# Perceiver block: time mixing in steps inside the attention of later batches, inverse square roots by power, first exponentials between score tiles

## Chip, cores and metric

The kernel runs on one core of a Trainium2 chip, in fp32. The metric is the device time of one execution in microseconds (us), the median of several runs. The engines are named as the profile names them: PE is TensorE (PEld its weight loads), DVE is VectorE, ACT is ScalarE, POOL is GpSimd, SP is SyncE, which here only issues DMAs. A line such as L357 is a line of the kernel before.

## The reference

A block of three residual parts over x, 32 batches of 64 tokens of 256 channels, with a context of 1601 keys of 192 channels for each batch. With LN a layer norm without weights (divide by the square root of the variance plus 1e-5):

```python
# 1. cross attention, 16 heads of 64
q = LN(x) @ w_q;  k, v = split(context @ w_kv)
x = x + softmax(q k^T / 8) v @ w_out + b_out
# 2. time mixing over the 64 tokens of a batch
z = LN(x);  s = z shifted by one token, zero first
k = (z*mix_k + s*(1-mix_k)) @ Wk.T      # v and r alike, with their own mix and weight
r = sigmoid(r)
td = exp(-exp(time_decay))
for t:                                   # num, den start at zero
    e   = exp(time_first + k_t)
    w_t = (num + e*v_t) / (den + e)
    num = td*num + exp(k_t)*v_t;  den = td*den + exp(k_t)
x = x + (r * w) @ Wo.T + bo
# 3. feed-forward, 1024 wide
x = x + relu(LN(x) @ w1 + b1) @ w2 + b2
```

## The kernel before

**Setup.** x is held in SBUF as 16 tiles of 128 tokens (two batches each, `x_sb`). The key projection is folded into the queries, so that scores are taken against the raw context: `queries` normalises x, multiplies by `w_q` and by the transposed key weights, and stores the folded queries to `q_dram` by SyncE (L233, L239) in four groups. The time-mixing weights are transposed (`rw_T`, L317). Nine small loads of biases and per-channel vectors (`bias_rows`, `cols`, `b1_sb`, L303 to L311) are issued by GpSimd.

**Attention** runs over 64 halves u = 2b + j, one batch b and eight heads j at a time, so that a half has 512 query columns. `scores` computes six tiles `s_ps` of 128 x 2 x 512 in PSUM (two buffers, L350) and a rest `s_ps_r` (L369); ScalarE copies each to `s_sb` (L357), VectorE keeps a running maximum (L359, L361). `hooks` are functions called after a given score tile. `max_all` reduces the maximum over partitions on GpSimd (L387), `exps` subtracts it on VectorE (L393) and takes exponentials on ScalarE (L396). `Half.total` sums the exponentials (VectorE, then GpSimd, L427); `inverse` turns the sums into reciprocals (L437 to L441). `av_lo` and `av_hi` multiply the exponentials by the raw context, low 128 channels (L450, `o_lo`) and high 64 (L462, L472, `o_hi`); `out` scales them (L488). After every fourth half, `vproj` applies the value weights (L504) and the output projection (L515) for one tile of 128 tokens and adds to `x_sb` (L522, L523).

The loop is a software pipeline written out by hand: TensorE's queue for half u is the score tiles of u, then `av_lo` of u-1, then `av_hi` of u-1. The previous half's inverse is the hook after score tile 3, `vproj` the hook after tile 1. The engines work through their queues in order; a scheduler places the instructions of different streams in each queue. Four halves, with one `vproj`, form a period; there are 16.

**The tail** starts when attention is done. It works on four blocks of 512 tokens. `rwkv(nb)` is the time mixing of a block: `normed` (statistics on VectorE, square root on ScalarE, reciprocal, and eight transposes, L599), the shifted copy `xp` (L607), for k, v and r a scaled copy `tmp` on ScalarE (L618) and a product-and-add `in_k`, `in_v`, `in_r` on VectorE (L621), the projections (L630) with N=512, exponentials (L651) and a sigmoid (L658), 32 scans per block (L663), the reciprocal of the denominator (L670), products (L671, L672) and the output product `ry` (L677). `ffn(nb)` is the feed-forward: `h_ps` (L698), relu, `fy` (L710), two adds (L718, L719) and the output DMA (L720). The order is written out:

```python
    rwkv(0)
    for nb in range(NB):
        if nb + 1 < NB:
            rwkv(nb + 1)
        ffn(nb)
```

The inverse square root of the norms is

```python
    def rstd_of(dst, var):
        nc.vector.tensor_scalar(dst, var, EPS, None, ALU.add)
        nc.scalar.activation(dst, dst, AF.Sqrt)
        nc.vector.reciprocal(dst, dst)
```

Of the kernel before, what the change touches and what calls it, by code (L numbers as in the profile page):

```python
# [9 lines left out]
F32 = mybir.dt.float32  # L10
# [10 lines left out]
def kernel(  # L21
# [33 lines left out]

    nc = tc.nc
# [27 lines left out]
    nc.gpsimd.memset(ones, 1.0)  # L84

# [11 lines left out]
    def rstd_of(dst, var):  # L97
        nc.vector.tensor_scalar(dst, var, EPS, None, ALU.add)
        nc.scalar.activation(dst, dst, AF.Sqrt)
        nc.vector.reciprocal(dst, dst)  # L100
# [12 lines left out]
    with tc.tile_pool(name="aw", bufs=1) as aw:  # L113
        wv_lo = aw.tile([P, INNER], F32, name="wv_lo")
        wv_hi = aw.tile([P, INNER], F32, name="wv_hi")
        wo_sb = aw.tile([P, INNER // P, D], F32, name="wo_sb")

        with ExitStack() as st_a:
            cpool = st_a.enter_context(tc.tile_pool(name="ctx", bufs=1))

            kp = st_a.enter_context(tc.tile_pool(name="keys", bufs=2))
# [140 lines left out]
            with tc.tile_pool(name="setup", bufs=1) as sp, tc.tile_pool(  # L262
# [20 lines left out]
                for n, w in (("Wk", Wk), ("Wv", Wv), ("Wr", Wr), ("Wo", Wo)):  # L283
                    nats[n] = sp.tile([P, 2, D], F32, name=f"nat_{n}")
                    nc.sync.dma_start(nats[n], w.rearrange("(c p) h -> p c h", p=P))
                for g in range(NP // 2):
# [14 lines left out]

                for n, v in enumerate((b_out, bo, b2)):
                    nc.gpsimd.dma_start(bias_rows[:, n, :], v.partition_broadcast(P))  # L303
                with nc.allow_non_contiguous_dma(reason="per-channel vectors"):
                    for n, v in enumerate((time_decay, time_first)):
                        nc.gpsimd.dma_start(cols[:, n, :], v.rearrange("(c p) -> p c", p=P))
                    for n, v in enumerate((mix_k, mix_v, mix_r)):
                        nc.gpsimd.dma_start(
                            cols[:, 2 + n, :], v.rearrange("a b (c p) -> p (a b c)", p=P)
                        )  # L310
                    nc.gpsimd.dma_start(b1_sb, b1.rearrange("(c p) -> p c", p=P))  # L311
# [20 lines left out]
            ap = st_a.enter_context(tc.tile_pool(name="attn", bufs=1))  # L332
            ps_s = st_a.enter_context(tc.tile_pool(name="ps_s", bufs=2, space=PSUM))
            ps_o = st_a.enter_context(tc.tile_pool(name="ps_o", bufs=1, space=PSUM))
            ps_m = st_a.enter_context(tc.tile_pool(name="ps_m", bufs=2, space=PSUM))

            def bank(shape, name):
                return ps_m.tile(shape, F32, tag="m", name=name)

# [50 lines left out]
            def exps(u, s_sb, mb):  # L390
                for i in range(KC // 4):
                    s4 = s_sb[:, 4 * i : 4 * i + 4, :]
                    nc.vector.tensor_tensor(  # L393
                        s4, s4, mb.unsqueeze(1).to_broadcast([P, 4, HALF]), ALU.subtract
                    )
                    nc.scalar.activation(s4, s4, AF.Exp)  # L396
                sr = s_sb[0:KR, KC, :]
                nc.vector.tensor_tensor(sr, sr, mb[0:KR, :], ALU.subtract)
                nc.scalar.activation(sr, sr, AF.Exp)

            class Half:
# [27 lines left out]
                def inverse(self):  # L429
# [10 lines left out]
                    self.rden = ap.tile([P, HALF // BL, BL], F32, tag="rden", name=f"rden_{u}")  # L440
# [89 lines left out]
            oT = None  # L530
            for u in range(2 * B):
                b, j = divmod(u, 2)

                hooks = {}
                if late is not None:
                    hooks[1] = [late.vproj]
                if last is not None:
                    hooks[3] = [last.inverse]

                if last is not None:  # L540
                    last.total()
# [7 lines left out]
                exps(u, s_sb, mb)  # L549
                if j == 0 and b + 1 < B:  # L550
                    cT_next = ctx_prep(b + 1)
                elif j == 1:
                    cT = cT_next
                if last is not None:
                    last.av_hi()
                    last.out()
                if j == 0:
                    c_tiles[b] = ctx_load(b)
# [4 lines left out]
            late.vproj()  # L563
            last.total()
            last.inverse()
            last.av_lo(0, NCK)
            last.av_hi()
# [3 lines left out]
    NB = 4  # L571
    TB = NT * P // NB
    BB = TB // T
    TT = TB // P
    NF = FF // P
    wp = ctx.enter_context(tc.tile_pool(name="fw", bufs=1))
    rp = ctx.enter_context(tc.tile_pool(name="rw", bufs=1))
    fp = ctx.enter_context(tc.tile_pool(name="ff", bufs=2))
    pp_t = ctx.enter_context(tc.tile_pool(name="pp_t", bufs=2, space=PSUM))
    pp_m = ctx.enter_context(tc.tile_pool(name="pp_m", bufs=4, space=PSUM))  # L580
    pp_y = ctx.enter_context(tc.tile_pool(name="pp_y", bufs=2, space=PSUM))

    w1_sb = wp.tile([P, 2, FF], F32, name="w1_sb")
    w2_sb = wp.tile([P, NF, D], F32, name="w2_sb")
    nc.sync.dma_start(w1_sb, w1.rearrange("(c p) f -> p c f", p=P))
    nc.sync.dma_start(w2_sb, w2.rearrange("(c p) d -> p c d", p=P))

    def normed(nb, name, dst):
        tiles = [nb * TT + k for k in range(TT)]
        mv, rstd = stats_of(fp, tiles, f"{name}_{nb}")  # L590
        xn = fp.tile([P, TT, D], F32, tag="xn", name=f"xn_{name}_{nb}")
        for k, i in enumerate(tiles):
            nc.vector.tensor_scalar(
                xn[:, k, :], x_sb[:, i, :], mv[:, k, 0:1], rstd[:, k : k + 1], ALU.subtract, ALU.mult
            )
        for c in range(2):
            pt = pp_t.tile([P, TT, P], F32, tag="t", name=f"xT_{name}_{nb}_{c}")
            for k in range(TT):
                nc.tensor.transpose(pt[:, k, :], xn[:, k, c * P : (c + 1) * P], ident)  # L599
            dst(c, pt)  # L600

    def rwkv(nb):
        xp = rp.tile([P, 2, BB, T + 1], F32, tag="xp", name=f"xp_{nb}", bufs=2)
        nc.gpsimd.memset(xp[:, :, :, 0:1], 0.0)

        def put(c, pt):
            nc.scalar.copy(  # L607
                xp[:, c, :, 1 : T + 1], pt.rearrange("p k (b t) -> p (k b) t", t=T)
            )

        normed(nb, "ln2", put)

        mixed = []
        for n, nm in enumerate(("k", "v", "r")):
            tmp = rp.tile([P, 2, BB, T], F32, tag="tmp", name=f"tmp_{nm}_{nb}", bufs=2)
            mi = rp.tile([P, 2, BB, T], F32, tag=f"in_{nm}", name=f"in_{nm}_{nb}", bufs=2)
            for c in range(2):
                nc.scalar.activation(  # L618
                    tmp[:, c], xp[:, c, :, 0:T], AF.Copy, scale=omm[:, n, c : c + 1]
                )  # L620
                nc.vector.scalar_tensor_tensor(  # L621
                    mi[:, c], xp[:, c, :, 1 : T + 1], cols[:, 2 + n, c : c + 1], tmp[:, c],
                    ALU.mult, ALU.add,
                )
            mixed.append(mi.rearrange("p c b t -> p c (b t)"))

        def proj(src, w, c, nm):
            ps = pp_m.tile([P, TB], F32, tag="mm", name=f"{nm}_ps_{nb}_{c}")
            for hc in range(2):
                nc.tensor.matmul(  # L630
                    ps,
                    lhsT=rw_T[w][:, hc, c * P : (c + 1) * P],
                    rhs=src[:, hc, :],
                    start=(hc == 0),
                    stop=(hc == 1),
                )
            return ps

        rw = rp.tile([P, 2, TB], F32, tag="rwv", name=f"rwv_{nb}", bufs=2)
        num = rp.tile([P, 2, BB, T + 1], F32, tag="num", name=f"num_{nb}")  # L640
        den = rp.tile([P, 2, BB, T + 1], F32, tag="den", name=f"den_{nb}")
        nc.gpsimd.memset(num[:, :, :, 0:1], 0.0)
        nc.gpsimd.memset(den[:, :, :, 0:1], 0.0)
        ek = rp.tile([P, 2, TB], F32, tag="ek", name=f"ek_{nb}")
        e = rp.tile([P, 2, TB], F32, tag="e", name=f"e_{nb}")
        ekv = rp.tile([P, 2, TB], F32, tag="ekv", name=f"ekv_{nb}")
        ev = rp.tile([P, 2, TB], F32, tag="ev", name=f"ev_{nb}")
        r = rp.tile([P, 2, TB], F32, tag="r", name=f"r_{nb}")
        for c in range(2):
            pk = proj(mixed[0], "Wk", c, "k")  # L650
            nc.scalar.activation(ek[:, c], pk, AF.Exp)  # L651
# [35 lines left out]
    def ffn(nb):  # L687
        xT = fp.tile([P, 2, TB], F32, tag="xT", name=f"xT_{nb}")

        def put(c, pt):  # L690
            nc.scalar.copy(xT[:, c, :], pt.rearrange("p k t -> p (k t)"))  # L691
# [84 lines left out]
```

## Time and profile before

| | |
|---|---|
| median of 3 runs | 2681.37 us (2679.87 to 2684.73) |
| the profiled execution's own time | 2677.39 us |
| its span | 2675.6 us |
| end of the last high sums (L472), begin of the tail | 2447.3 us |
| a half without `vproj`, start to start | 34.04 us |
| a period of four halves | 143.65 us |
| score tiles, rest, low sums, high sums of one half | 15.65, 1.29, 11.36, 5.73 us |
| ScalarE table loads | 16, of 1.28 us |

The span is the profiled execution from its first to its last instruction; the time of a run has a little more around it. In the page, a group's line gives the engine, the operation, the tile written and those read, the number of instructions, busy time and the mean of one in ns, and the idle time of its engine just before it with what ended it. In a time line, a row is the start in us, the duration of the (merged) instructions, engine, line, operation, tiles and count, and in brackets the idle time before it and the instruction that ended it. Matmuls in fp32 appear as two records each.

### The profile page before, as it was taken

How to read it: one execution, taken by the hardware profiler on the slowest of the kernel's cores; microseconds unless marked ns; L12 is line 12 of the kernel's file. 1: busy time of each engine (PE TensorE's matmuls, PEld its weight loads, DVE VectorE, ACT ScalarE, POOL GpSimd, SP SyncE). 2: the span in 40 equal slices, each digit the busy share in tenths (PEclk: the TensorE clock that was granted, in tenths of full speed). 3: DMA queues.
4: the chain of work that ended last, by engine and by line, in shares of the span. 5: the costliest groups of instructions: out<-in, count | busy, mean ns of one | idle time of the engine just before them, and what ended most of it. 6: DMA issues, size and time to landing. Idle time of an engine off the chain costs nothing.

```text
span 2675.6 us, 27667 instructions
## 1 busy us (share of the span) xinstructions
PE 2605.0 (97%) x11168; PEld 1192.6 (45%) x11168; DVE 1905.6 (71%) x2143; ACT 963.5 (36%) x926; POOL 329.6 (12%) x156
## 2 busy tenths in 40 slices
PE   7979999999999999999999999999999999999699
PEld 3334444444444444444444444444444444444366
DVE  4467677776767677767777776767677767776864
ACT  2333333333333333333333333333333333333242
POOL 1011111111111111111111111111111111110000
PEclk9999999999999999999999999999999999999899
DMA  8983233332333331333233333333332333100000
GB/s 204 277 155 61 39 62 62 62 60 45 62 62 62 62 61 44 61 60 58 44 62 62 55 55 57 62 62 62 58 60 48 62 53 56 34 19 32 1 15 16
DMA packets 435279, 169.26 MB, mean 63 GB/s; under 512 B 330192, under 2 KB 421360, under 8 KB 435152
## 3 DMA queue, kind: packets, MB, share of 16 engines
q1 hardware_dynamic: 434272, 166.05, 32.4%
q8 instruction: 87, 1.43, 0.2%
q0 software_dynamic: 336, 0.40, 0.1%
q10 hardware_dynamic: 544, 1.05, 0.1%
q14 instruction: 40, 0.33, 0.0%
HBM read 138.60 MB, written 27.26 MB: 62 GB/s over the span
## 4 chain that ended last, share of the span: by engine, by line
PE 92%; DVE 4%; DMA 1%; ACT 1%; issue 1%; SPq 1%; POOL 0%; DVEq 0%; POOLq 0%; ACTq 0%
PE s_ps L350 37%; PE o_lo L450 27%; PE o_hi L462 13%; PE s_ps_r L369 3%; PE y_ps L515 2%; PE v_ps L504 2%; PE fy L710 2%; PE q_ps L192 2%; PE h_ps L698 1%; PE o_hi L472 1%; DVE e L670 1%; PE ql_ps L208 1%; DMA q_dram<-q_hi 1%; PE qh_ps L223 0%; DVE num L663 0%
## 5 line engine op out<-in xcount | busy, mean ns | idle before, releaser
L350 PE MATMUL s_ps<-q,cT 64*128 64x512 f32 x4608 | 1012.6, 594 | 13.2 <-ACT s_sb L357 12.3
L450 PE MATMUL o_lo<-s_sb,c 128*128 128x512 f32 (+1 forms) x1664 | 731.4, 596 | 0.0
L357 ACT COPY s_sb<-s_ps 128x1024 f32<-128x1024 f32 x384 | 388.7, 1013 | 936.6 <-PE s_ps L350 926.5
L350 PEld LDWEIGHTS s_ps<-q,cT 64*128 64x128 f32 x4608 | 440.8, 187 | 548.9 <-issue 534.7
L396 ACT ACTIVATE s_sb<-s_sb 128x2048 f32<-128x2048 f32 x192 | 366.7, 1911 | 452.4 <-DVE s_sb L393 452.4
L393 DVE TENSOR_TENSOR s_sb<-s_sb,mb 128x2048 f32<-128x2048 f32 x192 | 428.6, 2288 | 100.8 <-POOL mb L387 100.8
L450 PEld LDWEIGHTS o_lo<-s_sb,c 128*128 128x128 f32 (+1 forms) x1664 | 311.4, 190 | 391.6 <-issue 391.2
L361 DVE TENSOR_TENSOR m<-m,s_sb 128x1024 f32<-128x1024 f32 x256 | 313.6, 1225 | 215.0 <-ACT s_sb L357 203.5
L462 PE MATMUL o_hi<-s_sb,c 128*64 128x512 f32 x1536 | 343.7, 596 | 0.0
L427 POOL PARTITION_ALL_REDUCE den<-sum x64 | 206.9, 3232 | 1062.7 <-DVE sum L423 1062.7
L421 DVE TENSOR_TENSOR t<-t,s_sb 128x1024 f32<-128x1024 f32 x256 | 312.5, 1221 | 13.2
L387 POOL PARTITION_ALL_REDUCE mb<-mx x64 | 114.1, 1783 | 1032.5 <-DVE mx L380 888.9
L462 PEld LDWEIGHTS o_hi<-s_sb,c 128*64 128x64 f32 x1536 | 104.8, 137 | 231.1 <-issue 206.8
L437 DVE STREAM_TRANSPOSE turned<-den 128x512 f32<-128x512 f32 x64 | 45.5, 711 | 199.9 <-POOL den L427 199.9
L369 PE MATMUL s_ps_r<-q,cT 64*65 64x256 f32 x768 | 93.6, 376 | 0.0
L257 DVE STREAM_TRANSPOSE cT<-cb 128x768 f32<-128x768 f32 x96 | 92.6, 967 | 0.0
L359 DVE TENSOR_TENSOR m<-s_sb 128x1024 f32<-128x1024 f32 x64 | 75.7, 1183 | 7.8 <-ACT s_sb L357 7.8
L419 DVE TENSOR_TENSOR t<-s_sb 128x1024 f32<-128x1024 f32 x64 | 77.7, 1214 | 0.0
L369 PEld LDWEIGHTS s_ps_r<-q,cT 64*65 64x65 f32 x768 | 54.1, 134 | 52.7 <-issue 33.5
L192 PE MATMUL q_ps<-xnT,wq_sb 128*128 128x512 f32 x128 | 60.0, 611 | 0.0
L515 PE MATMUL y_ps<-wo_sb,outT 128*128 128x256 f32 x256 | 59.5, 386 | 0.0
L698 PE MATMUL h_ps<-xT,w_sb 128*128 128x512 f32 x128 | 56.1, 594 | 0.6 <-ACT xT L691 0.6
(125 smaller groups left out, 1482.7 us busy)
## 6 DMA issues: line engine op xcount, KB each, us to landing
q<-q_dram SPq DMA_DIRECT2D x64, 768.0 KB, 6.8
c<-in_ctx_dram SPq DMA_DIRECT2D x32, 1152.0 KB, 6.2
cb<-in_ctx_dram SPq DMA_DIRECT2D x192, 104.0 KB, 4.3
cb<-in_ctx_dram SPq DMA_DIRECT2D x192, 96.0 KB, 3.3
q_dram<-q_lo SPq DMA_DIRECT2D x16, 1024.0 KB, 8.8
q_dram<-q_hi SPq DMA_DIRECT2D x32, 256.0 KB, 6.8
x_sb<-in_x_dram SPq DMA_DIRECT2D x4, 512.0 KB, 8.3
w_sb<-in_L_ffn_w_dram SPq DMA_DIRECT2D x2, 1024.0 KB, 4.9
```

The costliest lines, as they stand in the source:

```text
L192: nc.tensor.matmul(pq, lhsT=wq_sb[:, c, hp * P : (hp + 1) * P], rhs=xnT[:, c, :], start=(c == 0), stop=(c == 1),)
L350: nc.tensor.matmul(ps[:, k, :], lhsT=cT[rs, s, i * P : (i + 1) * P], rhs=q[rs, s, js : js + HALF], start=(s == 0), stop=(s == NS - 1),)
L357: nc.scalar.copy(s_sb[:, 2 * i : 2 * i + 2, :], ps)
L361: nc.vector.tensor_tensor(m2, m2, s_sb[:, 2 * i : 2 * i + 2, :], ALU.max)
L369: nc.tensor.matmul(ps[0:KR, k, 0:HH], lhsT=cT[rs, s, NB1 * BL : KT + 1], rhs=q[rs, s, js + k * HH : js + (k + 1) * HH], start=(s == 0), st ...
L387: nc.gpsimd.partition_all_reduce(mb, mx, P, bass_isa.ReduceOp.max)
L393: nc.vector.tensor_tensor(s4, s4, mb.unsqueeze(1).to_broadcast([P, 4, HALF]), ALU.subtract)
L396: nc.scalar.activation(s4, s4, AF.Exp)
L421: nc.vector.tensor_tensor(t2, t2, p[:, 2 * i : 2 * i + 2, :], ALU.add)
L427: nc.gpsimd.partition_all_reduce(self.den, self.sum, P, bass_isa.ReduceOp.add)
L450: nc.tensor.matmul(self.po, lhsT=self.ctx[0:n, self.at[c], 0:P], rhs=self.s_sb[0:n, c, :], start=(c == 0), stop=(c == NCK - 1),)
L462: nc.tensor.matmul(self.ph[o * C2 : (o + 1) * C2, :], lhsT=self.ctx[:, self.at[c], P:C], rhs=self.s_sb[:, c, :], start=(c < 2), stop=False ...
```

## The change

- `rstd_of`: VectorE adds epsilon as before, then GpSimd raises to the power -0.5 (`root` is a tile of -0.5). Square root and reciprocal go.
- The sigmoid becomes an exponential: `er` = exp(-r), and the quotient is ev / ((1 + er)(den + e)), with one reciprocal. The one multiplication by r goes.
- Time mixing is a class `Mixing` that works on one tile of 128 tokens, i = 0 to 15. For tiles 0 to 14 its steps are spread over the attention of later halves: `norm` after `out` in u = 4i+5, in which `vproj` of tile i ran; `mix` as the hook after score tile 2 of u = 4i+6; `project` (Wk, Wv) between `av_lo` and `av_hi` in u = 4i+7; `gate` (Wr) and `scan` after `out` of the same; its `out` as the hook after score tile 2 of u = 4i+8 (of tile 14 between the last half's `av_lo` and `av_hi`). The scaled copies `tmp` for k, v and r and the later `e` share one buffer (tag `e`). Projections have N=128, the output product N=256; all PSUM tiles of these steps come from the two buffers of `ps_m`, as those of `vproj` do.
- The tail is four `ffn` with N=512; the norms of the next block and the steps of tile 15 are called between product tiles. `pp_t` has one buffer for two, `pp_m` three for four; `ps_m` stays.
- `exps` returns its four parts as functions. Those of half 0 are hooks after score tiles 2 to 5 of half 1; `total` and `inverse` of half 0 follow after half 1's own exponentials. The other halves run their parts at once.
- The nine small loads move from GpSimd to SyncE, ahead of the first query store.
- Pools are opened in another order; the feed-forward weights lie over the pool of keys and queries, and the value and output weights are freed with attention.

The core of the diff:

```diff
     def rstd_of(dst, var):
         nc.vector.tensor_scalar(dst, var, EPS, None, ALU.add)
-        nc.scalar.activation(dst, dst, AF.Sqrt)
-        nc.vector.reciprocal(dst, dst)
+        nc.gpsimd.tensor_tensor(dst, dst, root[:, 0 : dst.shape[1]], ALU.pow)
...
+                for n, v in enumerate((b_out, bo, b2)):
+                    nc.sync.dma_start(bias_rows[:, n, :], v.partition_broadcast(P))
...
+            class Mixing:
...
+                def mix(self):
+                    i = self.i
+                    pt = bank([P, 2, 2, T], f"xT_ln2_{i}")
+                    for c in range(2):
+                        nc.tensor.transpose(pt[:, c, :, :], self.xn[:, c * P : (c + 1) * P], ident)
+                    xp = rp.tile([P, 2, 2, T + 1], F32, tag="xp", name=f"xp_{i}")
+                    nc.gpsimd.memset(xp[:, :, :, 0:1], 0.0)
+                    nc.scalar.copy(xp[:, :, :, 1 : T + 1], pt)
+                    self.mixed = []
+                    for n, nm in enumerate(("k", "v", "r")):
+                        tmp = rp.tile([P, 2, 2, T], F32, tag="e", name=f"tmp_{nm}_{i}")
+                        mi = rp.tile([P, 2, 2, T], F32, tag=f"in_{nm}", name=f"in_{nm}_{i}")
+                        for c in range(2):
+                            nc.scalar.activation(
+                                tmp[:, c], xp[:, c, :, 0:T], AF.Copy, scale=omm[:, n, c : c + 1]
+                            )
+                            nc.vector.scalar_tensor_tensor(
+                                mi[:, c], xp[:, c, :, 1 : T + 1], cols[:, 2 + n, c : c + 1],
+                                tmp[:, c], ALU.mult, ALU.add,
+                            )
...
+                def proj(self, n, w):
+                    ps = bank([P, 2, 2, T], f"{w}_ps_{self.i}")
+                    for c in range(2):
+                        for hc in range(2):
+                            nc.tensor.matmul(
+                                ps[:, c, :, :],
+                                lhsT=rw_T[w][:, hc, c * P : (c + 1) * P],
+                                rhs=self.mixed[n][:, hc, :],
...
+                def gate(self):
+                    i = self.i
+                    pr = self.proj(2, "Wr")
+                    self.er = rp.tile([P, 2, 2, T], F32, tag="in_r", name=f"er_{i}")
+                    nc.scalar.activation(self.er, pr, AF.Exp, scale=-1.0)
...
+                    nc.vector.scalar_tensor_tensor(
+                        self.e, self.er, 1.0, self.e, ALU.add, ALU.mult
+                    )
+                    nc.vector.reciprocal(self.e, self.e)
...
             for u in range(2 * B):
...
+                phase, i = (u - 5) % 4, (u - 5) // 4
+                mixer = mixing.get(i)
+                if phase == 1 and mixer:
+                    hooks[2] = [mixer.mix]
+                elif phase == 3 and mixer:
+                    hooks[2] = [mixer.out]
+                if u == 1:
+                    hooks = {i + 2: [part] for i, part in enumerate(parts)}
+                elif last is not None:
                     last.total()
...
-                exps(u, s_sb, mb)
+                parts = exps(s_sb, mb)
+                for part in parts if u else ():
+                    part()
...
+                if phase == 2 and mixer:
+                    mixer.project()
                 if last is not None:
                     last.av_hi()
                     last.out()
+                if phase == 2 and mixer:
+                    mixer.gate()
+                    mixer.scan()
+                elif phase == 0 and i >= 0:
+                    mixing[i] = Mixing(i)
+                    mixing[i].norm()
...
+        mixer = Mixing(NT - 1)
+        xTs = {0: normed(0)}
+        mixer.norm()
...
+        steps = (
+            [mixer.mix, norms[1], mixer.project, mixer.gate],
+            [mixer.scan, norms[2], mixer.out],
+            [norms[3]],
+            [],
+        )
+        for nb in range(NB):
+            ffn(nb, xTs[nb], list(steps[nb]))
```

## The prediction, made before the changed kernel ran

> **What bounds the kernel now.** I read the page's busy shares first, then the chain that ended last, then stretches of the span, and last the time lines of single attention halves.
>
> ```profile
> PE 2605.0 (97%) x11168; PEld 1192.6 (45%) x11168; DVE 1905.6 (71%) x2143; ACT 963.5 (36%) x926; POOL 329.6 (12%) x156
> ...
> PE 92%; DVE 4%; DMA 1%; ACT 1%; issue 1%; SPq 1%; POOL 0%; DVEq 0%; POOLq 0%; ACTq 0%
> ```
>
> Two stretches, each with its length, then busy PE, PEld, DVE, ACT and POOL, the TensorE clock, the DMA share and GB/s:
>
> ```profile
> 207.43:351.08 143.65, 143.65 (x634) 64.49 (x634) 107.21 (x106) 52.83 (x46) 20.06 (x8) 1.00 0.30 58
> 2447.33:2675.60 228.27, 189.86 (x688) 118.68 (x684) 146.35 (x375) 77.00 (x118) 1.27 (x12) 0.93 0.06 19
> ```
>
> TensorE carries 92% of the chain. The first stretch is a period of four halves: TensorE is busy in all 143.65 us. Whatever the change gives TensorE there lengthens the span. The second is the tail after the last high sums: TensorE idles 38 us of 228 and runs at 0.93 of its clock. The waits of TensorE say where:
>
> ```profile
> PE ry L677 <- DVE rwv L672: 15.4, 3, 12.3
> ...
> PE s_ps L350 <- ACT s_sb L357: 12.3, 2, 11.0
> PE k_ps L630 <- DVE in_k L621: 12.2, 4, 5.7
> PE xT_ln L599 <- DVE xn_ln L593: 5.5, 1, 5.5
> ```
>
> Three of the four are time mixing in the tail, behind VectorE's four 6.55 us reciprocals (L670); the second is one 10.95 us wait near the start, in which ScalarE loads a table and takes the first exponentials.
>
> **What the Trainium skill says.** "ScalarE: Activation LUTs", What ACT_TABLE_LOAD costs: a change of function set is a load of about 1283 ns; the trace has 16, 1.28 us each, twelve of them in the tail. "TensorE: Matmul & The Clock Gate", What's actually happening: an idle window of about 3.4 us, free-running, halves the clock until a busy one. The trace agrees in kind: with TensorE idle from 2454.5 the clock is halved from about 2457.1, and about 4 us of work then run at half. "GPSIMD Engine Reference", 2.1 Instruction dispatch: the first call to a freshly loaded GpSimd library costs about 6 us (5.95). The trace has only one exposed: 12.27 us before the identity's affine select at 14.45, while all DMA engines are full, which allows 6 but shows twice that.
>
> **The change, part by part.** S is the start of a half's scores.
>
> *1. TensorE work moved into attention.* In each of 15 periods (four halves, one tile of 128 tokens): two transposes, 12 projections with N=128, two output products with N=256. The tail's projections come in two records each, 8 records of N=512 in 3.60 us; N=128 should take 0.11 each by length, but 128-column loads cannot be faster than the transposes, 0.12 each. So 24 x 0.12 = 2.9. The output products: 16 records in 3.7, so 4 x 0.23 = 0.9. Transposes 0.25. Together 4.05 us, all on the path: x15 = **+61** (58 by length; +85 if each record takes the 0.19 us of a weight load).
>
> *2. The mix step's queue.* It stands after score tile 2 of the second half of a period and puts, on ScalarE, a copy and six scalings (L618's work) **ahead of the copies of score tiles 3 to 5**. The three scaled tiles share one buffer, so the second pair waits for VectorE's products of the first, and the third for those of the second. VectorE reaches the first product only behind the softmax inverse and two maxima. The half at S=2218.51 shows when:
>
> ```profile
> 2227.31 0.71 DVE L437 STREAM_TRANSPOSE turned<-den 128x512 f32<-128x512 f32 x1 [3.44 <-POOL den L427]
> ...
> 2228.98 1.18 DVE L359 TENSOR_TENSOR m<-s_sb 128x1024 f32<-128x1024 f32 x1
> 2230.26 3.88 DVE L361 TENSOR_TENSOR m<-m,s_sb 128x1024 f32<-128x1024 f32 x3
> ```
>
> and ScalarE's copy of tile 3:
>
> ```profile
> 2229.06 1.01 ACT L357 COPY s_sb<-s_ps 128x1024 f32<-128x1024 f32 x1 [1.56 <-PE s_ps L350]
> ```
>
> The inverse waits for GpSimd's sum over partitions; the second maximum ends at 2230.26 + 1.29, S+13.0. Then products to S+13.55, second scalings to 14.3, products to 14.6, third scalings to 15.3 (0.3 to 0.39 us each by the section on table loads just named, 186 ns + 0.833 N + 93 for a pointer; the trace's 0.73 for 512 columns fits), and the copy of tile 3, 1.01, to S+16.3; today it starts at S+10.55. TensorE's tile 5 takes tile 3's bank, since there are two, and would start at S+13.1. So TensorE stalls 2.6 to 3.5 us; I take 3.15: x15 = **+47**. Nothing hides it: VectorE and ScalarE have slack later in the half, but TensorE's queue is in order. The stall is about as long as an idle window, so some may halve the clock at about 2 us each: +4 (0 to +30).
>
> *3. Products and scans.* VectorE gains about 9 us in 144 (an estimate from the tail's rows at a quarter of their columns) where it has 36 idle; the new exponentials stand behind the half's own. The output product waits 0.2 to 0.5 us for the reciprocal (256 columns by 6.55/4 = 1.64) and the gating multiply at the end of VectorE's half: 14 x 0.35 = **+5** (0 to +8).
>
> *4. Square root by power on GpSimd.* In the changed program each power in attention has a library change before it and another before the next all-reduce: two per period. In the first half of a period GpSimd is free between these:
>
> ```profile
> 2180.18 3.23 POOL L427 PARTITION_ALL_REDUCE den<-sum  x1 [15.80 <-DVE sum L423]
> ...
> 2190.11 0.42 DVE L523 TENSOR_TENSOR x_sb<-x_sb,bias_rows 128x256 f32<-128x256 f32 x1
> ...
> 2204.79 1.78 POOL L387 PARTITION_ALL_REDUCE mb<-mx  x1 [21.39 <-DVE mx L380]
> ```
>
> From 2183.41 to 2204.79 are 21.4 us; with 0.6 for the power, two changes fit if one takes up to 10.4. At the page's 6 all is hidden, VectorE's wait for the power too (it is idle until 2193.49). At the 12 of the start the maximum is 3 to 3.4 late, the exponentials with it, and as they stand before the next half's score copies and its mix step, TensorE loses about that: **0**, upper end +45 to +50. A gain is excluded: GpSimd had nothing there before.
>
> *5. The tail.* What is left after the last high sums: value and output projection 7.15 (2447.33 to 2454.48); two transposes of block 0 with a single bank 2.65; four feed-forwards of 14.00 + 13.81 = 111.2; the other 24 transposes 2.7; tile 15's mixing 4.05; a short wait for its normalised input 1; from the last product to the end 3.75. Sum 132.5 against 228.3: **-96** (-92 to -99). It assumes VectorE's norms and tile 15's scan, some 25 us in all, run under the 14 us groups of products, and relu (0.6 per tile of 1.75) as before. Three product banks in place of four cost nothing at that rate; the table loads vanish with the waits they stood in.
>
> *6. First exponentials.* Between the second half's score tiles, without a table load: the second score copy comes after two of the four exponentials, so tile 3 still waits about 7 us instead of tile 2 10.95, with the same clock loss. First sums at 185.9 instead of 190.27: **-4.4** (-7 to -1).
>
> *7. Nine loads from SyncE.* About 0.6 us of issue each, 5.6 us ahead of the first query store (32.69). SyncE's queue idles from 44.7 to 59.7, but four-byte elements fill DMA engines that are full then: **+1** (-1 to +6). GpSimd's queue loses what delayed nothing.
>
> Sum: 61 + 47 + 4 + 5 + 0 - 96 - 4.4 + 1 = **+17.6**. The profiled execution took 2677.39 (span 2675.6), so 2695; it was 4.0 under the median of the runs, 2681.37, so 2699.
>
> **Rivals.**
> - *The mix stall stays away (faster).* If VectorE's first product ran before S+10.1, tile 3's copy would end by S+13.1 and TensorE would wait for nothing: 2699 - 47 - 4 = **2648**. The whole change breaks even where the stall is about 2.0 us, first product near S+11.8. For it: VectorE idles 3.44 us just before the inverse, so an earlier sum would move everything up. Against it: in the changed program's order on VectorE the products stand behind that inverse and two maxima.
> - *The library change shows (slower still).* At 12 us each, 2699 + 45 = **2744**. For it: the only exposed change here. Against: that one shared the DMA engines with the input loads, while attention uses 0.30 of them.
> - *Loading bounds the short projections:* 0.19 for each record, +24, **2723**. The value projection's N=128 records with 64 columns come at 0.055, which speaks against.
> - *The tail isn't only feed-forward:* the norms or tile 15 keep their waits, say half of the 38 us idle in the tail: about **2718**.
>
> **How the numbers follow.** The likeliest case, 0.66, with its own range 2675 to 2728: terms 1, 2 and 5 are uncertain by 10 or so each. The short-projection and tail rivals 0.10 together, the library rival 0.13, the faster rival 0.11. The forecast is 2699; the range 2672 to 2745 leaves out most of the faster rival and a tenth besides. A measurement of this kernel tells about 0.2%, 5.4 us, from no change. The likeliest case falls within that for about 0.1 and below it hardly; so faster 0.12, same 0.11, slower 0.77.
>
> **What would show it.** Right: periods of about 151 us in place of 143.65; in each, score tile 5 of the second half waiting about 3 us for ScalarE's copy, with that copy behind scalings that wait for VectorE; a tail of about 132 us with TensorE nearly full; ScalarE without a table load in the tail. Wrong: a mix half without that wait (then faster), the all-reduce of the first half later than S+28 (the library), projections slower than 0.13 us a record, or feed-forwards separated by waits.

## The result, and the profile after

The changed kernel took 2709.19 us (median of 4 runs, 2708.15 to 2709.42) against 2681.8 of the kernel before in the same comparison: ratio 1.0103, 95% interval 1.0087 to 1.0119. It is slower by 27 us. The profiled executions stand 32.0 us apart (spans 2707.6 and 2675.6), since that of before was one of its faster ones; the accounts below are of spans.

The busy shares and the chain of the changed kernel, as on the page before:

```profile
PE 2636.1 (97%) x11456; PEld 1219.4 (45%) x11456; DVE 1920.0 (71%) x2283; ACT 962.4 (36%) x1019; POOL 342.1 (13%) x176
...
PE 77%; DVE 14%; POOL 3%; ACT 2%; DMA 2%; issue 2%; SPq 1%; DVEq 0%; POOLq 0%; ACTq 0%
```

TensorE's share is as high as before, but the chain that ended last now leaves it: VectorE and GpSimd have 17% of it, where they had 4%. A chain of waits runs through the attention that was not there. Two stretches, a period and the tail after the last high sums (length, busy PE, PEld, DVE, ACT, POOL, clock, DMA share, GB/s):

```profile
2138.12:2291.17 153.05, 150.32 (x664) 68.54 (x662) 114.31 (x130) 56.16 (x57) 20.83 (x10) 0.99 0.30 54
2576.20:2707.60 131.40, 125.66 (x528) 85.78 (x524) 36.42 (x114) 30.95 (x53) 4.63 (x5) 1.00 0.05 17
```

The tail fell from 228.3 to 131.4 us. The period grew from 143.65 to 153.05, and TensorE is idle in 2.7 of it. The waits of TensorE between the first low sums and the tail are a single line (total, times, longest):

```profile
PE s_ps L466 <- ACT s_sb L473: 39.2, 15, 2.7
```

and this is one of the fifteen, on TensorE:

```profile
2187.58 0.44 PE L361 MATMUL xT_ln<-ident,xn_ln 128*128 128x128 f32 x2
2187.95 5.42 PE L466 MATMUL s_ps<-q,cT 64*128 64x512 f32 x24
2196.10 4.54 PE L466 MATMUL s_ps<-q,cT 64*128 64x512 f32 x12 [2.73 <-ACT s_sb L473]
```

on ScalarE:

```profile
2189.08 0.69 ACT L370 ACTIVATE tmp_k<-xp,omm 128x128 f32<-128x128 f32 x2
2193.35 0.69 ACT L370 ACTIVATE tmp_v<-xp,omm 128x128 f32<-128x128 f32 x2 [3.57 <-DVE in_k L373]
2194.46 0.69 ACT L370 ACTIVATE tmp_r<-xp,omm 128x128 f32<-128x128 f32 x2 [0.42 <-DVE in_v L373]
2195.06 1.91 ACT L473 COPY s_sb<-s_ps 128x1024 f32<-128x1024 f32 x2
```

and on VectorE:

```profile
2188.60 0.71 DVE L556 STREAM_TRANSPOSE turned<-den 128x512 f32<-128x512 f32 x1 [3.45 <-POOL den L546]
...
2191.56 1.23 DVE L477 TENSOR_TENSOR m<-m,s_sb 128x1024 f32<-128x1024 f32 x1
2192.70 0.61 DVE L373 SCALAR_TENSOR_TENSOR in_k<-xp,cols,tmp_k 128x128 f32<-128x128 f32 x2
2193.78 0.64 DVE L373 SCALAR_TENSOR_TENSOR in_v<-xp,cols,tmp_v 128x128 f32<-128x128 f32 x2 [0.47 <-ACT tmp_v L370]
```

The half starts at S=2179.66. VectorE's first product comes at S+13.04, behind the inverse that waits for GpSimd and behind two maxima; only then may ScalarE write `tmp_v`, 3.57 us after it was ready. The copies of score tiles 3 and 4 follow at S+15.4, and TensorE's tile 5 starts at S+16.44. The second thing to see is the duration in TensorE's third row, 4.54 us. One period earlier the same tile, after the same wait, took 2.85:

```profile
2044.75 2.85 PE L466 MATMUL s_ps<-q,cT 64*128 64x512 f32 x12 [2.73 <-ACT s_sb L473]
```

The clock that the profile shows as granted is 1.00 over that tile and 0.61 over the one at 2196.10: there it reads 0.50 from about 2196.5 to 2199.9. Half of these 3.4 us, 1.7 us, is what the tile lost.

### The profile page after: what moved, and what is told of

The parts are those of the page before. It is cut to its first block, busy times and chain, and to the rows that moved or that the text cites. A ratio compares the mean times of both kernels' runs of the same rounds, so it can differ in the third digit from the quotient of the medians.

```text
span 2707.6 us, 28505 instructions
## 1 busy us (share of the span) xinstructions
PE 2636.1 (97%) x11456; PEld 1219.4 (45%) x11456; DVE 1920.0 (71%) x2283; ACT 962.4 (36%) x1019; POOL 342.1 (13%) x176
## 4 chain that ended last, share of the span: by engine, by line
PE 77%; DVE 14%; POOL 3%; ACT 2%; DMA 2%; issue 2%; SPq 1%; DVEq 0%; POOLq 0%; ACTq 0%
PE s_ps L466 30%; PE o_lo L569 21%; PE o_hi L581 10%; DVE s_sb L513 4%; DVE t L540 3%; PE s_ps_r L485 2%; PE fy L766 2%; PE y_ps L634 2%; PE v_ps L623 2%; PE h_ps L752 2%; POOL den L546 2%; PE q_ps L195 2%; DVE m L477 1%; ACT s_sb L473 1%; POOL mb L503 1%
## 5 line engine op out<-in xcount | busy, mean ns | idle before, releaser
L466 PE MATMUL s_ps<-q,cT 64*128 64x512 f32 x4608 | 1043.3, 604 | 50.0 <-ACT s_sb L473 49.1
L514 ACT ACTIVATE s_sb<-s_sb 128x2048 f32<-128x2048 f32 (+1 forms) x256 | 400.6, 1589 | 472.3 <-DVE s_sb L513 472.3
L513 DVE TENSOR_TENSOR s_sb<-s_sb,mb 128x2048 f32<-128x2048 f32 (+1 forms) x256 | 466.8, 1886 | 103.4 <-POOL mb L503 103.4
```

The source lines that it names most:

```text
L466: nc.tensor.matmul(ps[:, k, :], lhsT=cT[rs, s, i * P : (i + 1) * P], rhs=q[rs, s, js : js + HALF], start=(s == 0), stop=(s == NS - 1),)
L513: nc.vector.tensor_tensor(s, s, m, ALU.subtract)
L514: nc.scalar.activation(s, s, AF.Exp)
```

## Experiments

Theory A: the scaled copies' single buffer makes ScalarE wait for VectorE, the score copies queue behind it, TensorE waits for the bank, and this wait costs more than its length because the clock is halved after it. Rival B: the seven ScalarE operations cost, whether they wait or not. Rival C: the time is TensorE's added products.

**Three buffers for the scaled copies.**

```diff
-                        tmp = rp.tile([P, 2, 2, T], F32, tag="e", name=f"tmp_{nm}_{i}")
+                        tmp = rp.tile([P, 2, 2, T], F32, tag=("num", "den", "e")[n], name=f"tmp_{nm}_{i}")
```

> The scaled copies tmp_k, tmp_v and tmp_r of the mix step get three buffers (those of num, den and e, which are dead at that time) in place of one; nothing else changes. Theory A (the shared buffer makes ScalarE wait for VectorE, the score copies behind it come late, TensorE waits 2.73 us in each of 15 mix steps, and the clock is halved after 10 of them): score tile 3's copy ends by about S+12.6, before tile 5 is due at S+13.1; 15 x 2.73 and 10 x 1.7 go, 2709 - 56 = 2653 (2648 to 2662). Rival B (it is the seven ScalarE operations ahead of the score copies that cost, not their wait): at least half of the wait stays, 2680 or more. Rival C (the time is TensorE's own new matmuls): 2700 to 2709.

Measured: 2647.76 us, ratio to before 0.9881 (0.9864 to 0.9897), so 61 us off, and 32 us under the kernel before in the same comparison. By the traces 60.2 us of it lie between the first low sums and the tail (2387.1 us in the changed kernel, 2326.9 here), the rest in the start. ScalarE in this kernel's mix step (S=1980.20):

```profile
1989.62 0.69 ACT L370 ACTIVATE tmp_k<-xp,omm 128x128 f32<-128x128 f32 x2
1990.22 0.68 ACT L370 ACTIVATE tmp_v<-xp,omm 128x128 f32<-128x128 f32 x2
1990.80 0.68 ACT L370 ACTIVATE tmp_r<-xp,omm 128x128 f32<-128x128 f32 x2
1991.39 1.01 ACT L473 COPY s_sb<-s_ps 128x1024 f32<-128x1024 f32 x1
```

The seven operations are all there, back to back, and the copy of tile 3 starts at S+11.2. B falls, and so does C as the account of these 61 us: the operations and the products are all still there, and what went is the wait with the clock behind it, worth about 60 us where A had 56. What the added products cost by themselves comes with the run without time mixing.

**Two buffers.**

```diff
+                        tmp = rp.tile([P, 2, 2, T], F32, tag=("e", "num", "e")[n], name=f"tmp_{nm}_{i}")
```

> Two buffers for the scaled copies: tmp_k and tmp_r share one, tmp_v has that of num. ScalarE waits for VectorE once in place of twice. Theory A: TensorE's wait shrinks from 2.73 by the 1.1 us of one round to about 1.6 us; if the clock is halved only by waits near the length of its window, no halving is left: 2709 - 15 x 1.1 - 17 = 2676 (2670 to 2682). If a wait of 1.6 us halves it as often as one of 2.7: about 2692. Rival B: as in the run with three buffers, 2690 or more. Rival C: 2705 to 2709.

Measured: 2674.82 us, ratio 0.9982 (0.9975 to 0.9989). One round of waiting is left:

```profile
2016.81 2.85 PE L466 MATMUL s_ps<-q,cT 64*128 64x512 f32 x12 [1.61 <-ACT s_sb L473]
```

TensorE waits 1.61 us, and the tile then takes 2.85: no halved clock, in any of fourteen such waits (in the last period there is none). So the last 1.1 us of waiting cost 34 us in 15 periods, of which the waiting itself is 17; the halved clock is the other half. It is not shown that a wait of 1.6 us can never halve the clock: the fourteen come at equal distances of 150.23 us, and in the changed kernel the halvings follow a fixed order, two tiles halved and one not, through all fourteen waits of 2.73 us. These are repetitions of a few positions in time, not independent trials.

**The mix step after score tile 5.**

```diff
-                    hooks[2] = [mixer.mix]
+                    hooks[5] = [mixer.mix]
```

> One shared buffer as in the changed kernel, but the mix step stands after score tile 5 of its half in place of tile 2: only the copy of the rest tile is behind it on ScalarE. Theory A: the same waits between ScalarE and VectorE, but nothing of TensorE hangs on them: its wait of 2.73 us goes, the maximum comes some 2 us later and the exponentials with it, which the next half covers: 2653 to 2662. Rival B: about the same as A here, as the seven operations no longer stand ahead of score copies. Rival C: 2705 to 2709. If the late maximum reaches TensorE: 2670 to 2690.

Measured: 2648.0 us, ratio 0.9881 (0.9866 to 0.9896), as with three buffers. The shared buffer is still waited for (ScalarE 0.76 us before `tmp_v`), but no bank hangs on it. The scheduler slipped the rest tile's copy in between the scaled copies, so the first exponential starts at S+25.0 where it was S+23.9 in the kernel before: 1.1 us later, not the 2 I had put. What cost was the wait ahead of the score copies, not the wait as such.

**No time mixing in attention** (tiles 0 to 14 left out).

```diff
-                    mixing[i] = Mixing(i)
-                    mixing[i].norm()
+                    pass
...
-            mixing[NT - 2].out()
```

> Leaves out the time mixing of tiles 0 to 14 altogether (norm, mix, project, gate, scan and output product; so x goes to the feed-forward without it), tile 15's in the tail stays. It shows the price of these steps within attention: by the traces 130 us from the first low sums to the last high sums, so 2709 - 130 = 2579 (2574 to 2584), with periods of 143.65 us again. If the new start, the loads or the pools also slow attention, more stays: 2585 or above.

Measured: 2579.35 us, ratio 0.9626 (0.9612 to 0.964), with periods of 143.65 us. Against three buffers this prices the mixing that waits for nothing: 68 us by the medians, 72 by the spans (2646.1 and 2574.0). The rest of the 130 us between this run and the changed kernel is the wait and the clock.

The other four start from the kernel with three buffers, at 2647.76.

**Square root on ScalarE again.**

```diff
-        nc.gpsimd.tensor_tensor(dst, dst, root[:, 0 : dst.shape[1]], ALU.pow)
+        nc.scalar.activation(dst, dst, AF.Sqrt)
+        nc.vector.reciprocal(dst, dst)
```

> On top of the kernel with three buffers for the scaled copies (2648): the inverse square root is again ScalarE's Sqrt and VectorE's reciprocal, as in the kernel before; so GpSimd needs no library change in attention, and ScalarE instead two table loads of 1.28 us in each period and some in the tail. Theory A (both are hidden in attention: the loads of a period fall in ScalarE's waits, the library changes between two all-reduces): attention unchanged; the first exponentials may pay one load on the start's path and the tail one or two: 2648 to 2653. Rival D (the library changes cost TensorE something that the waits don't name): below 2645. Rival E (a table load in front of score copies or exponentials reaches TensorE): 15 x 1.3 = 20 more, about 2668.

Measured: 2647.37 us, ratio 0.9877 (0.9861 to 0.9894): no difference. The starts of the two versions differ, so the stretch from the first low sums to the tail is the better test: it is 2326.86 us in both. Two table loads in each period are hidden as well as two library changes were; D and E fall. GpSimd's rows in the changed kernel show no library change of their own, but there is room for one between the end of the sum over partitions and the power, 7.5 us later:

```profile
2141.99 3.23 POOL L546 PARTITION_ALL_REDUCE den<-sum  x1 [16.40 <-DVE oT L607]
2152.72 0.60 POOL L102 TENSOR_TENSOR rstd_ln<-rstd_ln,root 128x1 f32<-128x1 f32 x1 [7.49 <-DVE rstd_ln L101]
2166.05 1.81 POOL L503 PARTITION_ALL_REDUCE mb<-mx  x1 [12.73 <-DVE mx L496]
```

The power and the maximum start when VectorE's operand comes, and the maximum does so 27.9 us after its half began at 2138.12, as in the kernel before (2204.79, in a half that began at 2176.91). The sum waits for something that the description of the change does not name: the reciprocals `rden` now lie in the buffer of `den`, so GpSimd may write the new sums only when VectorE has read the old reciprocals (`oT`). In the mix half the sum still waits for its own operand, so this has no part in the stall.

**First exponentials at once.**

```diff
-                if u == 1:
-                    hooks = {i + 2: [part] for i, part in enumerate(parts)}
-                elif last is not None:
+                if last is not None:
                     last.total()
```

> On top of the three buffers: half 0's exponentials run at once, before half 1's score copies on ScalarE, and its total and inverse follow as in the kernel before; there is still no table load before them. Theory A: TensorE's third score tile of half 1 waits again for the last of the four exponentials, 10.95 - 1.3 for the table load = 9.6 us in place of 7.14, with the clock halved either way: +2.5, 2650 (2648 to 2653). If the placing between the tiles itself brought nothing: 2647 to 2648. If it cost (the sums of half 0 come later): below 2646.

Measured: 2651.53 us, ratio 0.9888 (0.9873 to 0.9903); the span is 2646.5 against 2646.1. TensorE's wait for the first exponentials is 8.43 us against 7.13. The sign is that of A, but the ratio's interval overlaps that of the three buffers (0.9864 to 0.9897). A gain of the placing of 1 to 2 us, as the ratios and the wait suggest, is not shown.

**The nine loads on GpSimd again.**

```diff
-                    nc.sync.dma_start(bias_rows[:, n, :], v.partition_broadcast(P))
+                    nc.gpsimd.dma_start(bias_rows[:, n, :], v.partition_broadcast(P))
```

(the other six alike, at the place they had before)

> On top of the three buffers: the nine bias and column loads are issued by GpSimd again, where the kernel before had them. Theory A (it was GpSimd's own DMA issue, not a library change, that held the identity's affine select until 14.45 before): affine select back near 14 us from 1.4, TensorE's first transposes wait 14.8 us in place of 8.4; but setup is bound by DMA, so scores start only about 1 us later: 2648 to 2651. Rival F (it was a library load at the start): affine select stays near 1.4 us and the time at 2648. Rival G (the small loads on SyncE delay the query stores): below 2646.

Measured: 2643.13 us, ratio 0.9859 (0.9844 to 0.9874). The span is 4.3 us shorter and the scores start at 138.81 in place of 142.12, as rival G had it. Kernels with the same setup start them between 140.23 and 142.12, so 1.4 to 3.3 us of it go with the loads' place. The ratio's interval overlaps that of the three buffers, so the gain rests on the traces and is not clear of noise in the times. It is the fastest version that does all the work, 37 us under the kernel before. A fails: the affine select started at 2.57 us and not near 14, behind one of GpSimd's own DMA issues (1.35 to 2.21 us) and with 0.36 us of waiting. F was near on the select (1.4 us), but had 2648 for the time.

**The gate product with the other projections.**

```diff
                     mixer.project()
+                    mixer.gate()
...
-                    mixer.gate()
                     mixer.scan()
```

> On top of the three buffers: the gate product (Wr) directly after the projections Wk and Wv, ahead of the high sums. Theory A (there are two banks of ps_m; Wr needs that of Wk, which is free only when ScalarE has taken both exponentials of Wk, some 2.1 us after Wv has ended by the trace): TensorE waits about 1.7 us in each of 15 periods, less 0.1 for one change of stream fewer: 2648 + 24 = 2672 (2665 to 2678). Rival H (the place of the gate makes no difference): 2645 to 2649.

Measured: 2680.49 us, ratio 0.9999 (0.9991 to 1.0008): 31 to 33 us lost, by spans and by medians, where A had 24. The order of TensorE in that half:

```profile
2067.91 1.07 PE L581 MATMUL o_hi<-s_sb,c 128*64 128x512 f32 x2
2070.07 1.16 PE L383 MATMUL Wr_ps<-in_r,Wr_T 128*128 128x128 f32 x8 [1.09 <-ACT e L401]
2071.16 4.93 PE L581 MATMUL o_hi<-s_sb,c 128*64 128x512 f32 x21
```

The scheduler let one high-sum product go first, and the gate waits 1.09 us for the bank of Wk. That is 16 us in all. The half grew by 2.16 us, 15 x 2.16 = 32, so as much again is left. I put it down to the lone product, which no run tries apart from the wait. The 24 records of the high sums otherwise take 5.30 us, 0.22 each; the program writes them in turn to the two halves of `o_hi`, 64 columns each. The product that was cut off took about 0.43 for each record, and one record is left without a partner at the end. So of the two places for the gate, that behind the high sums is the better one.

## Why the prediction was right or wrong

The direction, the mechanism and the range (2672 to 2745) were right; the time was 10 us low, and against the change of the spans (+32.0) the sum of 17.6 was 14 short. That it came this near is partly luck: step 1 and the clock were about 22 us too low together, and the wait and step 3 about 9 too high.

| step | predicted | measured |
|---|---|---|
| 1. TensorE's added work | +61 | +70.5 |
| 2. wait of the mix step | +47 | +43 |
| 2. halved clock | +4 | +17 |
| 3. output product waits | +5 | 0 |
| 4. library changes | 0 | 0 |
| 5. tail | -96 | -96.9 |
| 6, 7. start | -3.4 | -1.2 |

*Step 1* was mis-sized. With three buffers a period's halves are 34.61, 36.91 and 35.30 us long where each was 34.04: 0.57 for the transposes, 2.87 for the projections, 1.26 for the output product, together 4.70 and not 4.05. Eight records of the projections are 0.89 us, 0.11 each and not 0.12, so weight loads don't bound them and that rival falls. What was missing came to 0.3 us each at the transposes and the output product; at the projections the shorter records hid about 0.1 at each of two places. I put this down to the change from one stream of products to another; it is what is left after the records, and no row shows it alone.

*Step 2* had every link: the shared buffer, the first product at S+13.0 (measured S+13.04), the bank of tile 3. The wait is 2.73 us in 14 periods and 1.00 in the last, 39.2, and about 0.26 to restart each time. It is shorter than my 3.15 because TensorE comes to tile 5 at S+13.71 and not at S+13.1: the step's own transposes stand ahead of it. The wrong term is the clock. In ten of the fifteen mix steps tile 5 took 4.33 to 4.54 us, in the others 2.85: 1.7 us, ten times. My +4 at 2 us each stands for two of fifteen, since the Trainium skill ("TensorE: Matmul & The Clock Gate", What's actually happening) gives an idle window of about 3.4 us. The measurement decides: 2.73 us of idle time are enough in 10 of 14 cases, 1.61 never in fourteen. The figures that I had quoted showed it already: TensorE idle from 2454.5 and the clock halved from about 2457.1 are 2.6 us, less than the wait of 3.15 that I expected.

*Step 3:* the gating multiply ended at 2263.09 and the output product started at 2263.80, behind score tile 2; TensorE's list of waits has none in it. *Step 4* held, and the square root's run shows that neither way costs. *Step 5* held to a microsecond: norms, scan and relu ran under the products, with 0.96 us of waiting for tile 15's input where I had put 1. *Steps 6 and 7* pulled against each other: the first score copy waits for a context load until 147.47 us before and 147.83 after, so scores that start 1.0 us earlier bring little, and by the run with the loads on GpSimd their place on SyncE took up to 3 us back. There is one more halving here: the third score tile of half 0 waits 2.77 us in place of 1.39, and the 48 records from there take 12.05 us in place of 10.57, so half 1 starts later, which takes back part of what the shorter wait for the first exponentials (7.14 us in place of 10.95) brings.

The faster rival named the right point. With the wait gone the changed kernel comes to 2648, which that rival had worked out for an earlier product; it was reached by giving ScalarE no reason to wait instead. That the two agree to the microsecond is luck: the rival's sum holds the same errors in steps 1, 3 and 6. The library, short-projection and tail rivals did not occur.

## What to carry to other kernels

Work put into the gaps of a pipeline should wait for nothing while it stands ahead of an eviction in an in-order queue: look for scratch tiles that share a buffer across two engines, and spread them over tiles that are dead at that time. Where TensorE has no idle time, price the added products at their records plus 0.1 to 0.3 us for every insertion, as it came out here, and price a wait of 2.7 us at its length plus up to 1.7 us of slow clock behind it. A lone product cut off from a sequence of half-width ones seems to cost about 1 us more, so such a sequence is better left whole.

## What the runs showed of the hardware that I had not expected

- TensorE's clock is halved after 2.73 us of waiting in 10 of 14 cases, in a fixed order of two halved and one not; after 1.61 us in none of 14, which come at equal distances. In the step shown the clock falls to 0.50 about 0.4 us after the work has started again and stays there for 3.4 us. Each halving costs about 1.7 us.
- The identity's affine select on GpSimd waited 12.27 us in the kernel before, and 10.58 with the square root on ScalarE, in both of which GpSimd's last work, small memsets aside, is a sum over partitions. Where its last work is a power, the select started at 1.38 or 2.57 us. That the library of the execution before is still there would explain it; it was not tried.
- Products of 64 columns ran at 0.22 us per record of 512 in an unbroken sequence that alternates between the two halves of `o_hi`, and at 0.43 when cut off from it.
